# Moving every slot's folds behind the next slot's broadcast of B

## The chip, the cores and the metric

The kernel runs on one core of one Trainium2 chip. The metric is the device time of one execution in microseconds. The five engines are named as the profile names them: PE (TensorE; its weight loads are PEld), DVE (VectorE), ACT (ScalarE), POOL (GpSimd) and SP (SyncE, which here only issues DMAs). Each engine runs its own instructions in order and waits for others through semaphores.

## The reference

Two layers work on x of shape (16, 96, 64, 64), float32. Layer 0 is a graph layer on windows of 8 x 8 positions; layer 1 is two Mamba blocks (selective scans) over the 4,096 positions of each image, followed by a fusion and a batch norm.

```python
# layer 0
y = affine(conv1x1(x, fc1_w, fc1_b), fc1_s, fc1_t)
nodes = window_partition(y, 8).reshape(Bw, C, 64).transpose(0, 2, 1)
idx = knn_idx(nodes, 9)                          # the nine nearest of 64
feat = concat([x_i, x_j - x_i]); h = einsum('bnkc,oc->bnko', feat, ew) + eb
h = max(gelu(h * es + et), axis=2)
x = affine(conv1x1(window_reverse(h), fc2_w, fc2_b), fc2_s, fc2_t) + x
# layer 1, twice: one Mamba block on seq of shape (16, 4096, 96)
h = layernorm(seq); xs, z = split(h @ in_w)      # 192 channels each
xc = silu(causal_conv4(xs) + conv_b)
dt, Bm, Cm = split(xc @ xproj_w)                 # 6, 16, 16
delta = softplus(dt @ dt_w + dt_b)
dA  = exp(delta[..., None] * A)                  # (16, 4096, 192, 16)
dBx = delta[..., None] * Bm[:, :, None, :] * xc[..., None]
hstates[l] = dA[l] * hstates[l - 1] + dBx[l]     # scan over the positions
y = einsum('blds,bls->bld', hstates, Cm) + Dp * xc
seq = seq + (y * silu(z)) @ out_w
# then a fusion product with the pooled mean of x, batch norm, + x
```

## The kernel before

A row is one image's stretch of 512 positions: 16 images times 8 rows. An item is one row in one of the two Mamba blocks, 256 items in all, ordered so that the two blocks alternate (block 1 works four rows behind block 0). The 16 states of an item are taken in eight pairs p = 0 to 7, two states for 64 channels on the 128 partitions, and the 192 channels as three column groups of 512. Item and pair together are one slot: 2,048 slots, numbered m, in one Python loop (line 951). Two items, 16 slots, repeat as a pattern with almost the same work, so a slot is named here by m % 16; p is m % 8. There are 128 patterns.

The order of work on each engine is the order in which the program writes it (a manual schedule). A slot does this for the scan:

- ACT computes da = exp(delta * a) for three column groups (L758, in `chosen`, which also issues the two DMAs that spread the row of C over the partitions into ct, L751). It runs one or two slots ahead, through `ahead`.
- PE spreads the pair's row of B over the partitions, into the one PSUM bank bt (L792, `bcast`). At the top of slot m it does so for slot m + 1. It may not overwrite bt before VectorE has read it.
- DVE scans slot m: hb = da * h + db, in two pieces (L990), and then multiplies u by bt for slot m + 1, giving db (L798, `times_b`, two pieces). There are three hb buffers, so scan m reuses the one of slot m - 3.
- POOL saves the last column (L1024), multiplies hb by ct in place (L1025), and writes the restart value for a later slot into the first column of u (L789).
- PE folds the product of slot m - 1 into y: `folded` (L814 and L816), four matmuls which sum the two states' halves and add to the PSUM tile y over the eight pairs.

y has one buffer. In slot p = 1 ACT copies the last item's finished y out (`emptied`, L823), and PE then starts the new y with the skip product (L808, L809).

Between these, each slot takes steps of other work from generators: layer 0 for a row ahead (L369 to L578), the norm and the products in front of an item (L632 to L734) and behind it (L841 to L861). Their matmuls stand on PE between the broadcast at the top of the slot and the fold at its end. Their PSUM results share one pool of two banks, and ACT reads nearly all of them: each product waits for ACT to free a bank, and ACT waits for the product. Softplus, gelu, silu and exp need table loads on ACT, so its order is also fixed by hand. Every eighth pattern carries the pooled mean of a finished image as well (L590, L597).

In slots p = 1 the fold is already put off: it is kept in `put_off` and issued in slot p = 2, behind that slot's broadcast.

Of the kernel before, what the change touches and what calls it, by code (L numbers as in the profile page):

```python
# [21 lines left out]
def tile_conv_knn_mamba(ctx: ExitStack, tc: tile.TileContext, w: dict, out: bass.AP):  # L22
# [313 lines left out]
    def half(h):  # L336
        return slice(h * CB, (h + 1) * CB)
# [246 lines left out]
    def pooled(b):  # L584

        mean = pr.tile([C, 1], F32, tag="mean1", name=f"mean1_{b}")
        nc.vector.reduce_sum(mean, means.pop(b), AX.X)
        yield
        pg = pm.tile([C, 1], F32, tag="mm", name=f"pg_{b}")
        nc.tensor.matmul(pg, lhsT=gpT, rhs=mean, start=True, stop=True)  # L590
        yield
        gp = pr.tile([C, 1], F32, tag="gp", name=f"gp_{b}")
        nc.scalar.activation(gp, pg, AF.Relu, bias=gp_b[:, 0, :], scale=1.0 / L)
        yield
        def product():
            ps = pm.tile([C, 1], F32, tag="mm", name=f"pg2_{b}")
            nc.tensor.matmul(ps, lhsT=fusT[:, 1, :], rhs=gp, start=True, stop=True)  # L597
            return ps

        apart(product, lambda ps: nc.scalar.copy(gcol[:, b : b + 1], ps))  # L600
        yield


    PIECES = ((0, 2), (2, NB3))
    LAG = 4
    NR = NB * NQ
# [13 lines left out]
    def norm(n):  # L620

        b, i, k = items[n]
        nm = f"{b}_{i}_{k}"
        seq = seqs[b, k]
        assert (b, k) in done
        hn = hns[n % NHN]
        if k == 0:
            nc.gpsimd.memset(hn[:, :HALO], 0.0)
        else:
            nc.gpsimd.tensor_copy(hn[:, :HALO], hns[place[b, i, k - 1] % NHN][:, Q:])  # L630
        pc = pm.tile([C, Q], F32, tag="mm", name=f"pc_{nm}")
        nc.tensor.matmul(pc, lhsT=cmat, rhs=seq, start=True, stop=True)  # L632
        sq = pr.tile([C, Q], F32, tag="sq", name=f"sqv_{nm}")
        nc.scalar.activation(sq, pc, AF.Square)  # L634
        yield
        ps = pm.tile([C, Q], F32, tag="mm", name=f"pvar_{nm}")
        nc.tensor.matmul(ps, lhsT=ones_cc, rhs=sq, start=True, stop=True)
        rs = pr.tile([C, Q], F32, tag="rs", name=f"rs_{nm}")
        nc.scalar.activation(rs, ps, AF.Ln, bias=eps_t[:C], scale=1.0 / C)
        nc.scalar.activation(rs, rs, AF.Exp, scale=-0.5)  # L640
        yield
        nc.gpsimd.tensor_tensor(hn[:C, HALO:], seq, rs, ALU.mult)
# [118 lines left out]
    def carry(n):  # L761

        _, i, k = items[n]
        b0 = made[n][6]
        u, delta = made[n][5], made[n][4]
        fresh = pr.tile([128, NB3, NPR], F32, tag="fresh", name=f"fresh_{n}")
        carried[n] = fresh
        if k:
            first = pr.tile([128, NB3, NPR], F32, tag="first", name=f"first_{n}")
            for c in range(NB3):  # L770
                nc.scalar.activation(first[:, c], a_neg[i][:, c], AF.Exp, scale=delta[:, c, 0:1])
        yield
        nc.gpsimd.tensor_tensor(
            fresh,
            u[:, :, 0:1].to_broadcast([128, NB3, NPR]),
            b0.unsqueeze(1).to_broadcast([128, NB3, NPR]),
            ALU.mult,
        )
        for part in range(2):
            if k:  # L780
                cols = bass.ts(part, NPR // 2)
                nc.gpsimd.tensor_tensor(first[:, :, cols], first[:, :, cols], states[i][:, :, cols], ALU.mult)
                nc.gpsimd.tensor_tensor(fresh[:, :, cols], fresh[:, :, cols], first[:, :, cols], ALU.add)
            yield
            yield
# [5 lines left out]
    def bcast(n, p):  # L791
        nc.tensor.matmul(bt[:, 1:], lhsT=bsel[:, p, :], rhs=made[n][2][:, 1:], start=True, stop=True)  # L792

    def times_b(n, p):
        parts = []
        for lo, hi in PIECES:
            db = pd.tile([128, hi - lo, Q], F32, tag=f"db{lo}", name=f"db{lo}_{n}_{p}")
# [13 lines left out]
    def folded(n, p, hb, y):  # L811

        for h in range(2):
            nc.tensor.matmul(y[half(h), 0], lhsT=fold, rhs=hb[:, h, :], start=False, stop=(p == NPR - 1))  # L814
        for h in range(2):
            nc.tensor.matmul(  # L816
                y[half(h), 1, :QH], lhsT=fold, rhs=hb[:, 2, bass.ts(h, QH)], start=False, stop=(p == NPR - 1)
            )

    def emptied(n, y):  # L820

        yc = zs.popleft()
        nc.scalar.copy(yc, y.rearrange("p s q -> p (s q)")[:, : Q + QH])  # L823
        return yc
# [60 lines left out]
    def several_at_once(g, pace):  # L885

        while True:
            made = 0
            while made < pace:
                step = next(g, g)  # L890
                if step is g:
                    return
                if step in (TABLE, SLOT):
                    break
                made += step is not SPARE
            yield step
# [18 lines left out]
    def ahead():  # L915
        if coming:
            t = coming.popleft()
            soon[t] = chosen(*t)
# [24 lines left out]
    y = behind = None  # L943
# [7 lines left out]
    for m, (n, p) in enumerate(order):  # L951
        b, i, k = items[n]
        nm = f"{b}_{i}_{k}"
        after = order[m + 1] if m + 1 < len(order) else None

        for layer0, r, pace in rows_at.pop(m, ()):
            steps = layer0(*divmod(r, NQ))
            going.append(several_at_once(steps, pace) if pace > 1 else steps)
        between.extend(later[0])
        later = [later[1], []]  # L960
        if p == 0 and k == 0:
            states[i] = pr.tile([128, NB3, NPR], F32, tag=f"state{i}", name=f"state_{nm}")
        if p == 0 and whole:
            going.append(pooled(whole.pop(0)))
        if p == 0 and n + 2 < NI:
            going.insert(0, norm(n + 2))
        if p == 4 and n + 2 < NI:
            preps.append(prelude(n + 2))
        if p == 6 and n + 1 < NI:
            going.append(carry(n + 1))  # L970
        ct, at = soon.pop((n, p))
        if after is not None:
            bcast(*after)
        if p == 2:
            folded(*put_off)


        while uses:
            uses.pop(0)()
        acts = list(opening)  # L980
        opening.clear()
        if not acts and between and p not in (0, 1):
            acts.append(between.popleft())
        if len(acts) > 1:
            acts.pop(0)()
        for act in acts:
            act()
        hb = pr.tile([128, NB3, Q], F32, tag="hb", name=f"hb_{nm}_{p}", bufs=3)
        for (lo, hi), part in zip(PIECES, db):
            nc.vector.tensor_tensor_scan(  # L990
                *(t.rearrange("p c q -> p (c q)") for t in (hb[:, lo:hi], das[at][:, lo:hi], part)), 0.0, ALU.mult, ALU.add
            )
        free.append(at)
        while late:
            if between:
                between.popleft()()
            else:
                late.pop(0)()
        if p == 1 and n:
            yc = emptied(n - 1, y)  # L1000
        if p == 7 and n:
            going.append(tail(n - 1))
        if p == 2:
            ahead()
        held = step_on(going)
        if p == 4:
            ahead()
        held |= step_on(preps)
        close_steps()
        if between and p in (4, 5):  # L1010
            between.popleft()()
        if after is not None:
            if p == NPR - 1:
                restart(*after)
            db = times_b(*after)
        if behind is not None:
            if p == 1:
                y = py.tile([128, 2, Q], F32, tag="y", name=f"y_{nm}")
                skipped(n, y)
                put_off = (*behind, y)  # L1020
            else:
                folded(*behind, y)
        if k + 1 < NQ:
            nc.gpsimd.tensor_copy(states[i][:, :, p : p + 1], hb[:, :, Q - 1 : Q])  # L1024
        nc.gpsimd.tensor_tensor(hb, hb, ct.unsqueeze(1).to_broadcast([128, NB3, Q]), ALU.mult)  # L1025
        if m + 2 < len(order) and p != NPR - 2:
            restart(*order[m + 2])
        if p == 1 and n:
            gate(n - 1, yc)
        behind = (n, p, hb)  # L1030
        while (not held or not soon) and len(soon) < AHEAD and coming:
            ahead()
# [68 lines left out]
```

## Time and profile before

| | |
|---|---|
| median of 3 runs | 12,521.8 us (12,520.07 to 12,522.95) |
| the profiled execution, as timed | 12,521.96 us |
| its span, first to last instruction | 12,520.2 us |
| mean granted TensorE clock | 0.984 |
| DVE: scans L990, products L798 | 6,944.1 us and 3,711.4 us busy |
| POOL: products with C, L1025 | 7,074.4 us busy, 3,454 ns each |
| PE: folds L814 and L816 | 2,179.7 us and 1,244.0 us busy |
| PE: broadcasts L792 | 796.0 us busy, 389 ns each; 180.0 us idle before them |
| DVE's idle time before L798 | 564.1 us |

A row of the timeline gives an instruction's start and length in microseconds, its engine, line and operation, what it writes and reads, and in brackets the engine's idle time before it with what ended it. A line of the waits gives an engine's instruction, what it waited for, the total in microseconds, how often, and the longest. Ends of matmuls are modelled and overlap the next start, so matmuls are measured here from start to start.

### The profile page before, as it was taken

How to read it: one execution, taken by the hardware profiler on the slowest of the kernel's cores; microseconds unless marked ns; L12 is line 12 of the kernel's file. 1: busy time of each engine (PE TensorE's matmuls, PEld its weight loads, DVE VectorE, ACT ScalarE, POOL GpSimd, SP SyncE). 2: the span in 40 equal slices, each digit the busy share in tenths (PEclk: the TensorE clock that was granted, in tenths of full speed). 3: DMA queues.
4: the chain of work that ended last, by engine and by line, in shares of the span. 5: the costliest groups of instructions: out<-in, count | busy, mean ns of one | idle time of the engine just before them, and what ended most of it. 6: DMA issues, size and time to landing. Idle time of an engine off the chain costs nothing. (4 is left out here: it accounts for less than half of the span.)

```text
span 12520.2 us, 169034 instructions
## 1 busy us (share of the span) xinstructions
PE 11019.7 (88%) x50504; PEld 4348.2 (35%) x50504; DVE 11646.8 (93%) x10589; ACT 10249.1 (82%) x16756; POOL 10022.4 (80%) x10148
## 2 busy tenths in 40 slices
PE   7989899898999999899999989989999898998972
PEld 2333333333333333333333333333333333333320
DVE  3999999999999999999999999999999999999995
ACT  6888888888888888888888888888888888888863
POOL 2888888888888888888888888888888888888882
PEclk9999999999999999999999999999999999999996
DMA  1333333333333333333333333333333333333336
GB/s 38 90 86 94 88 90 93 85 92 90 89 92 88 92 91 88 92 91 87 93 89 89 93 86 93 91 89 92 87 93 91 86 93 88 90 93 86 93 92 270
DMA packets 1221003, 1169.01 MB, mean 93 GB/s; under 512 B 631456, under 2 KB 762926, under 8 KB 1213936
## 3 DMA queue, kind: packets, MB, share of 16 engines
q1 hardware_dynamic: 1212720, 1132.88, 33.8%
q10 hardware_dynamic: 7360, 25.32, 0.5%
q8 instruction: 397, 6.50, 0.2%
q14 instruction: 526, 4.31, 0.1%
HBM read 640.79 MB, written 93.09 MB: 59 GB/s over the span
## 5 line engine op out<-in xcount | busy, mean ns | idle before, releaser
L1025 POOL TENSOR_TENSOR hb<-hb,ct 128x1536 f32<-128x1536 f32 x2048 | 7074.4, 3454 | 692.0 <-DMA ct<-cd 448.0
L990 DVE TENSOR_TENSOR_SCAN hb<-da,db 128x1024 f32<-128x1024 f32 (+1 forms) x4096 | 6944.1, 1738 | 4.2 <-ACT da L758 4.2
L798 DVE TENSOR_TENSOR db<-u,bt 128x1024 f32<-128x1024 f32 (+1 forms) x4096 | 3711.4, 952 | 564.1 <-PE bt L792 201.0
L758 ACT ACTIVATE da<-delta,a 128x511 f32<-128x511 f32 x6144 | 3946.1, 710 | 15.9 <-DVE hb L990 8.2
L814 PE MATMUL y<-hb,fold 128*64 128x512 f32 x8192 | 2179.7, 610 | 41.2 <-POOL hb L1025 41.2
L516 ACT ACTIVATE da<-t,eb,es 128x512 f32<-128x512 f32 x1536 | 1168.3, 776 | 714.0 <-PE t L508 453.3
L816 PE MATMUL y<-hb,fold 128*64 128x256 f32 x8192 | 1244.0, 382 | 0.0
L508 PE MATMUL t<-oh,vu 128*128 128x512 f32 x2048 | 1006.4, 613 | 28.2 <-ACT da L516 26.6
L816 PEld LDWEIGHTS y<-hb,fold 128*64 128x64 f32 x8192 | 593.0, 138 | 1191.2 <-issue 1191.2
L1024 POOL COPY state<-hb 128x3 f32<-128x3 f32 x1792 | 374.6, 209 | 766.4 <-DVE hb L990 731.0
L447 DVE TENSOR_REDUCE hq<-da 128x192 f32<-128x1536 f32 x512 | 891.6, 1742 | 91.3 <-ACT da L516 91.3
L792 PE MATMUL bt<-bparts,bsel 128*128 128x511 bf16 x2048 | 796.0, 389 | 180.0 <-DVE db L798 176.6
L659 PE MATMUL pj<-hn,conv_in 128*128 128x512 f32 x2048 | 934.7, 599 | 18.4 <-ACT gcol L600 8.8
L814 PEld LDWEIGHTS y<-hb,fold 128*64 128x64 f32 x8192 | 507.9, 137 | 1078.1 <-issue 695.3
L511 PE MATMUL t<-oh,vu 128*64 128x512 f32 x2048 | 560.8, 626 | 311.6 <-ACT da L516 309.0
L732 POOL TENSOR_TENSOR up<-sp,xc 128x768 f32<-128x768 f32 x256 | 464.1, 1813 | 443.1 <-ACT sp L721 442.9
L664 PE MATMUL pj<-hn,conv_in 128*64 128x256 f32 x4096 | 498.9, 385 | 259.0 <-ACT xc L671 258.8
L671 ACT ACTIVATE xc<-pj,conv_b 128x512 f32<-128x512 f32 (+1 forms) x512 | 297.0, 580 | 425.3 <-PE pj L664 400.4
L477 ACT ACTIVATE oh<-off 64x512 f32<-64x512 bf16 x1024 | 638.2, 623 | 6.4
L492 PE MATMUL pv<-ewT,y 96*64 96x192 f32 x2048 | 447.0, 342 | 143.8 <-ACT sqv L634 83.2
L659 PEld LDWEIGHTS pj<-hn,conv_in 128*128 128x128 f32 x2048 | 378.6, 190 | 406.0 <-issue 368.7
L508 PEld LDWEIGHTS t<-oh,vu 128*128 128x128 f32 x2048 | 371.9, 193 | 394.9 <-issue 298.5
(188 smaller groups left out, 15801.1 us busy)
## 6 DMA issues: line engine op xcount, KB each, us to landing
ct<-cd SPq DMA_DIRECT2D x4096, 128.0 KB
delta<-sp SPq DMA_DIRECT2D x1024, 128.0 KB
u<-up SPq DMA_DIRECT2D x1024, 128.0 KB
delta<-sp SPq DMA_DIRECT2D x1024, 64.0 KB
u<-up SPq DMA_DIRECT2D x1024, 64.0 KB
x<-in_x SPq DMA_DIRECT2D x128, 192.0 KB
rn<-r4d SPq DMA_DIRECT2D x128, 192.0 KB
x_d<-x SPq DMA_DIRECT2D x128, 192.0 KB
```

The lines of the kernel that those rows point to most:

```text
L447: nc.vector.tensor_reduce(out(), g.rearrange("p s (i k) -> p s i k", k=KO), AX.X, ALU.max)
L477: nc.scalar.activation(ohs[p][0:NN, h], off[half(h)], AF.Relu, bias=1.0, scale=-1.0)
L508: nc.tensor.matmul(t, lhsT=vus[p][:, part, :128], rhs=ohw[part], start=True, stop=True)
L516: nc.scalar.activation(g, t, AF.Gelu, bias=e_b[:, j : j + 1], scale=e_s[:, j : j + 1])
L659: nc.tensor.matmul(ps, lhsT=wt[:, t, :128], rhs=hn[:, off : off + Q], start=(t == 0), stop=(t == taps - 1))
L758: nc.scalar.activation(da[:, c, 1:Q], delta[:, c, 1:], AF.Exp, scale=a_neg[i][:, c, p : p + 1])
L792: nc.tensor.matmul(bt[:, 1:], lhsT=bsel[:, p, :], rhs=made[n][2][:, 1:], start=True, stop=True)
L798: nc.vector.tensor_tensor(db, made[n][5][:, lo:hi], bt.unsqueeze(1).to_broadcast([128, hi - lo, Q]), ALU.mult)
L814: nc.tensor.matmul(y[half(h), 0], lhsT=fold, rhs=hb[:, h, :], start=False, stop=(p == NPR - 1))
L816: nc.tensor.matmul(y[half(h), 1, :QH], lhsT=fold, rhs=hb[:, 2, bass.ts(h, QH)], start=False, stop=(p == NPR - 1))
L990: nc.vector.tensor_tensor_scan(*(t.rearrange("p c q -> p (c q)") for t in (hb[:, lo:hi], das[at][:, lo:hi], part)), 0.0, ALU.mult, ALU.add)
L1025: nc.gpsimd.tensor_tensor(hb, hb, ct.unsqueeze(1).to_broadcast([128, NB3, Q]), ALU.mult)
```

## The change

In every slot the fold is kept back and issued in the next slot, behind that slot's broadcast, as it was in slots p = 1 alone. `HASTE` names the slots (m % 16) in which it is kept back, here all of them; the last slot, which has no broadcast after it, folds at once. What the other engines are given, and in which order, is not touched.

```diff
+    HASTE = {0,1,2,3,4,5,6,7,8,9,10,11,12,13,14,15,}
+    put_off = []
     PIECES = ((0, 2), (2, NB3))
...
         if after is not None:
             bcast(*after)
-        if p == 2:
-            folded(*put_off)
-
+        while put_off:
+            folded(*put_off.pop())
...
             if p == 1:
                 y = py.tile([128, 2, Q], F32, tag="y", name=f"y_{nm}")
                 skipped(n, y)
-                put_off = (*behind, y)
-            else:
-                folded(*behind, y)
+            put_off.append((*behind, y))
+            if p != 1 and (m % 16 not in HASTE or after is None):
+                folded(*put_off.pop())
```

## The prediction

> **What bounds the kernel now.** I read the page's busy shares first, then the waits of every engine against every other, then who waits for the scan, and then the timeline of one pattern of 16 slots (the pattern that begins at 6298.03 us), engine by engine. I then took the same rows for all patterns.
>
> The page:
> ```profile
> PE 11019.7 (88%) x50504; PEld 4348.2 (35%) x50504; DVE 11646.8 (93%) x10589; ACT 10249.1 (82%) x16756; POOL 10022.4 (80%) x10148
> ```
> VectorE (DVE) is the busiest at 93%, which by itself would make it the bound. The waits (engine and line, what it waited for, us in total, times, longest) say otherwise:
> ```profile
> ACT da L516 <- PE t L508: 453.3, 281, 3.3
> ACT xc L671 <- PE pj L664: 400.4, 254, 3.0
> ...
> ACT sqv L634 <- PE pc L632: 255.6, 146, 2.0
> PE pj L664 <- ACT xc L671: 259.4, 231, 1.6
> ...
> DVE db L798 <- PE bt L792: 201.0, 131, 11.4
> PE bt L792 <- DVE db L798: 176.6, 190, 3.4
> ```
> ScalarE and TensorE wait for each other for over 1,000 us. Who waits for VectorE's scan (L990)?
> ```profile
>   ACT da L758: 8.2, 3
>   ACT da L516: 5.0, 3
> ```
> ScalarE waited for it 13 us in the whole run. So the loop ScalarE to TensorE to ScalarE hardly looks at VectorE. The rows confirm it. Over 120 patterns (the 3rd to the 122nd of 128) I measured from the first L634 of a pattern to the first gelu of slot 2 (L516): 11.64 us at the 10th, 50th and 90th percentile alike; then to the gelu of slot 3: 4.42, to L721: 4.54, to L671: 6.88 and 2.73, all without spread. 105 patterns, less five with a half-rate TensorE clock, take 93.89 us on average, 93.38 to 93.97 between the 10th and 90th percentile. Every eighth pattern also carries the pooled-mean products (L590, L597) and takes 98.84. VectorE has about 4.2 us of idle time in a pattern before L798: 1.66 in slot 0, 0.89 in slot 3, 0.70 in slot 7, 0.20 in slot 8, 0.60 in slots 11 and 12. That idle time is slack: VectorE is put back in step once a pattern, in slot 7, where L798 waits for GpSimd's restart column, which hangs on ScalarE's L771 and on a transfer of C behind ScalarE's L721.
>
> **The change part by part.** The timeline of TensorE in slots 15 and 0:
> ```profile
> 6298.03 0.38 PE L792 MATMUL bt<-bparts,bsel 128*128 128x511 bf16 x1 [0.51 <-DVE db L798]
> 6298.67 1.10 PE L369 MATMUL pf<-x,fc1T 96*96 96x512 f32 x2 [0.27 <-ACT off L471]
> 6300.02 1.10 PE L557 MATMUL pf<-x,ident 96*96 96x512 f32 x2 [0.25 <-ACT dbl L689]
> ...
> 6305.51 1.08 PE L814 MATMUL y<-hb,fold 128*64 128x512 f32 x4
> 6306.42 0.60 PE L816 MATMUL y<-hb,fold 128*64 128x256 f32 x4
> 6306.95 0.39 PE L792 MATMUL bt<-bparts,bsel 128*128 128x511 bf16 x1
> 6307.18 1.02 PE L632 MATMUL pc<-x,cmat 96*96 96x512 f32 x2
> ```
> Here L369 and L557 wait for ScalarE; the next broadcast comes 1.44 us after the fold begins; L632, for which ScalarE waits 1.95 us, follows. And slots 10 and 11, where slot 10 already has its fold behind the broadcast:
> ```profile
> 6360.07 0.38 PE L792 MATMUL bt<-bparts,bsel 128*128 128x511 bf16 x1 [0.56 <-DVE db L798]
> 6360.38 1.08 PE L814 MATMUL y<-hb,fold 128*64 128x512 f32 x4
> 6361.28 0.60 PE L816 MATMUL y<-hb,fold 128*64 128x256 f32 x4
> 6361.82 1.98 PE L508 MATMUL t<-oh,vu 128*128 128x512 f32 x4
> 6365.26 1.08 PE L511 MATMUL t<-oh,vu 128*64 128x512 f32 x4 [1.46 <-ACT da L516]
> 6366.17 1.03 PE L814 MATMUL y<-hb,fold 128*64 128x512 f32 x4
> 6367.03 0.60 PE L816 MATMUL y<-hb,fold 128*64 128x256 f32 x4
> 6367.56 0.39 PE L792 MATMUL bt<-bparts,bsel 128*128 128x511 bf16 x1
> 6367.79 1.88 PE L508 MATMUL t<-oh,vu 128*128 128x512 f32 x4
> ```
>
> *What moves.* The same four matmuls of a fold change places with one broadcast in 14 of 16 slots; slots 2 and 10 (p = 2) have that order already. Orders on ScalarE, GpSimd and SyncE, and so every DMA issue, stay. VectorE's order stays; 1,789 scans gain a wait for TensorE.
>
> *What is gained.* The broadcast comes 1.39 to 1.44 us earlier (fold start to broadcast start) wherever VectorE is not the one it waits for. That cuts VectorE's idle time in slots 0, 11 and 12. I price it at nothing: what VectorE gains by slot 3 it waits out by slot 7. There L758's second column group ends only 0.48 us (median) before scan 7, and the restart column ends 0.03 us (median) before L798 starts. Both hang on ScalarE. The Trainium skill, Perfetto Trace Analysis, sections Identifying the Most-Contended Engine and Optimization Strategy, says to take the engine of highest occupancy and make what ends its gaps come sooner. By that rule the sum would be the gaps of slots 0, 3, 11 and 12, 3.15 us in 120 patterns, 378 us saved. The rows go against it here.
>
> *The swap itself.* Before: last L511 pass to fold 0.42, fold to broadcast 1.39, broadcast to next 0.23, together 2.04. After, from slots 2 and 10: 0.42, broadcast to fold 0.31, fold to next 1.44, together 2.17. After L846 it is 0.52 + 1.44 + 0.23 = 2.19 against about 2.18. So slot 3, where L508 of the next slot ends ScalarE's wait of 1.69, costs 0.13 us: 120 x 0.13 = 16 us, on the path.
>
> *A broadcast that waits for VectorE with the fold queued behind it.* This is the main cost. The broadcast may start 0.05 us after the L798 pair ends (the row of slot 10). Then come 0.31 and 1.44, so the next product starts at the earliest 1.80 us after that pair ends. Before, the fold ran inside that wait. Call x the time from the end of the L798 pair to the broadcast's start in the trace of before; the next product then started at x + 0.23, so it is late by 1.57 - x.
> - Slot 11: x is 1.21 at the median, and under 1.43 in 65% of the ordinary patterns. L508 is late by 0.44 us on average (the swap's own 0.13 is the least), and ScalarE's gelu waits for it.
> - Slot 8: x is 1.89 at the median; L632 is late in a third of the patterns, 0.15 us on average.
> - Slot 15: the fold goes in front of L369 and L557, which ScalarE releases. L557 can start at 1.80 + 0.94 (L369's two passes) = 2.74 us after the pair ends; it started at 2.50 at the median. Late by 0.30 us on average; L841 to L846, L632 and so ScalarE follow.
> - Slot 9 (x 0.95): late too, but ScalarE's L639 has about 0.5 us to spare there, so slot 11 covers it. Slot 7: L415 waits for ScalarE until after the fold. Elsewhere x is over 1.6.
>
> These don't add: once TensorE is late, the next broadcast waits less. Taking the latest of the three in each pattern gives 0.53 us in 105 patterns and 0.25 in the 15 with pooled means: 55.9 + 3.7 = 60 us. It comes back every pattern, since slot 7 ties VectorE to the late ScalarE again.
>
> *Clock.* The granted clock fell to half in slot 11 for 3.4 or 6.8 us in five of the 105 patterns, where TensorE had been busy for under half of the 3.41 us before. They took 95.5 us, 1.6 more. TensorE will now also stand at slot 11's broadcast, after the 1.46 us before L511; a dozen patterns are within 0.1 of that share. I take six more: 10 us (bounds 0, and 50 patterns: 80 us).
>
> *The new wait of the scan.* Scan m needs the buffer of fold m-3, now behind broadcast m. With the broadcast just in time the fold ends 1.82 us after the broadcast starts, and the scan starts 2.22 after it. Nothing, with 0.4 to spare. Scans 3 and 11 stand so already with no idle time. The y copy (L823) has 0.7 us between its last fold and its start. If either cover goes, the price is the excess: 0.1 us a scan on VectorE's slack, nothing on the path.
>
> *Folds that wait for GpSimd.* Only the last four patterns have them (40.9 us of TensorE's idle time after 11,800 us). There the broadcast no longer stands behind the fold: 4 x 0.7 = 3 us saved.
>
> *Sum.* The profiled execution took 12,521.96 us (span 12,520.2, and 1.8 around it), the median of the runs is 12,521.8. 12,522 + 16 + 60 + 10 - 3 = 12,605 us, 0.66% slower.
>
> **Rivals.**
> - *VectorE is the bound after all, and faster.* For it: 93%, and 201 us of waiting for the broadcast. The place is slot 7: if the restart column comes as much earlier as VectorE does (its product chain starts with the scan of slot 6), the 1.4 us of slot 0 last through the pattern, 120 x 1.4 = 168 us: 12,354; half of it 12,438. Against: the ct transfer and L771 there hang on ScalarE. It decides if L798's wait in slot 7 shrinks.
> - *The lateness is covered.* VectorE reaches slot 8 earlier by part of the 0.70 it waits in slot 7, broadcasts 8, 11 and 15 wait no more, and slots 3 and 11 cost 0.13 each: 120 x 0.26 = 31 us, 12,553; with the swap free, 12,522. For it: x varies by 0.7 to 2.1 in slot 11 (10th to 90th percentile) with that wait.
> - *The clock.* 50 patterns with a half-rate window: 12,675.
> - *The change does less than it says* is out: only slots 2 and 10, and the last fold, keep their places.
>
> **How the numbers follow.** Forecast, 12,555 to 12,670: 0.64. Covered, 12,520 to 12,555: 0.17; about 0.1 of this within 0.2% (25 us, what a measurement of this kernel can tell from no change). Faster: 0.12. Clock, over 12,670: 0.07. The range leaves out the clock case and most of the faster one: 12,510 to 12,670. Faster by over 0.2%: 0.12; within: 0.12; slower: 0.76.
>
> **What would show it.** Right: L798's idle time to the broadcast falls under 100 us; scans, which had 4.2 us, now wait for ScalarE's L758 in slot 7, some 50 to 120 us; TensorE's idle time before L792 rises from 180 to 300 or more; L369 and L557 no longer wait for ScalarE; 105 patterns of 94.4 to 94.7 us; ScalarE's wait in slot 11 for L508 grows. Wrong: the stretch from L557 to L634 and from L516 to L516 in slot 11 keeps its length, or the pattern becomes shorter than 93.9.

## The result, and the profile after

The changed kernel takes 12,723.8 us (median; 12,714.2 to 12,728.3) against 12,520.9 us for the kernel before, measured beside it: a ratio of 1.0161, 95% interval 1.0148 to 1.0173. It is 1.6% slower. The forecast was 12,605 us, 0.66% slower, with a range up to 12,670: the direction was right, the loss was two and a half times as large, and it lies outside the range.

The profiled execution took 12,728.3 us (span 12,726.6, mean granted clock 0.981). Lines move by one or two: the broadcast is now L794, the products of B L800, the fold L816 and L818, the scan L991. From the page, the busy shares and three of its groups:

```profile
PE 11366.1 (89%) x50504; PEld 4252.9 (33%) x50504; DVE 11735.9 (92%) x10589; ACT 10263.4 (81%) x16756; POOL 10015.6 (79%) x10148
...
L991 DVE TENSOR_TENSOR_SCAN hb<-da,db 128x1024 f32<-128x1024 f32 (+1 forms) x4096 | 6941.7, 1736 | 28.6 <-ACT da L760 19.4
L800 DVE TENSOR_TENSOR db<-u,bt 128x1024 f32<-128x1024 f32 (+1 forms) x4096 | 3717.7, 953 | 654.9 <-POOL u L791 342.7
...
L794 PE MATMUL bt<-bparts,bsel 128*128 128x511 bf16 x2048 | 791.8, 387 | 284.6 <-DVE db L800 273.2
```

TensorE does the same 50,504 matmuls, but is busy for 346 us more. The waits (us in total, times, longest) have grown where ScalarE waits for L508 and L634, where the broadcast waits for VectorE, and where VectorE waits for GpSimd's restart column:

```profile
ACT da L516 <- PE t L508: 545.5, 270, 3.9
...
ACT xc L673 <- PE pj L666: 399.0, 254, 2.7
...
DVE db L800 <- POOL u L791: 342.7, 346, 9.1
...
ACT sqv L636 <- PE pc L634: 303.3, 194, 2.7
...
PE bt L794 <- DVE db L800: 273.2, 386, 5.9
...
PE pj L666 <- ACT xc L673: 200.9, 231, 1.3
...
DVE db L800 <- PE bt L794: 154.8, 173, 11.0
```

Before, L508 kept ScalarE for 453 us, L632 (now L634) for 256 and L664 (now L666) for 400, the broadcast waited for VectorE 177, and VectorE waited for the restart column 131. The timeline of TensorE at the place that the prediction shows, slots 15 and 0 of the same pattern:

```profile
6398.44 0.38 PE L794 MATMUL bt<-bparts,bsel 128*128 128x511 bf16 x1 [0.88 <-DVE db L800]
6398.75 1.08 PE L816 MATMUL y<-hb,fold 128*64 128x512 f32 x4
6399.66 0.60 PE L818 MATMUL y<-hb,fold 128*64 128x256 f32 x4
6400.19 1.10 PE L369 MATMUL pf<-x,fc1T 96*96 96x512 f32 x2
6401.12 1.06 PE L557 MATMUL pf<-x,ident 96*96 96x512 f32 x2
```

The broadcast waits for VectorE, the fold stands behind it, and L369 and L557, which used to wait for ScalarE, now start 1.75 and 2.68 us after the broadcast instead of 0.64 and 1.99. Slots 10 and 11:

```profile
6461.86 0.38 PE L794 MATMUL bt<-bparts,bsel 128*128 128x511 bf16 x1 [0.34 <-DVE db L800]
6462.17 1.08 PE L816 MATMUL y<-hb,fold 128*64 128x512 f32 x4
6463.08 0.60 PE L818 MATMUL y<-hb,fold 128*64 128x256 f32 x4
6463.61 1.98 PE L508 MATMUL t<-oh,vu 128*128 128x512 f32 x4
6466.87 1.08 PE L511 MATMUL t<-oh,vu 128*64 128x512 f32 x4 [1.28 <-ACT da L516]
6467.88 0.39 PE L794 MATMUL bt<-bparts,bsel 128*128 128x511 bf16 x1
6468.20 1.08 PE L816 MATMUL y<-hb,fold 128*64 128x512 f32 x4
6469.11 0.60 PE L818 MATMUL y<-hb,fold 128*64 128x256 f32 x4
6469.64 1.99 PE L508 MATMUL t<-oh,vu 128*128 128x512 f32 x4
```

No wait stands between L511 and the second L508, and still they are 2.77 us apart (6466.87 to 6469.64); before it was 2.53 (6365.26 to 6367.79). L508 itself takes 1.99 instead of 1.88. ScalarE, at the same place, waits for it 1.68 us before (first row) and 2.03 us after (second and third):

```profile
6368.85 1.64 ACT L516 ACTIVATE da<-t,eb,es 128x512 f32<-128x512 f32 x2 [1.68 <-PE t L508]
...
6468.00 0.78 ACT L516 ACTIVATE da<-t,eb,es 128x512 f32<-128x512 f32 x1 [0.51 <-PE t L511]
6470.81 1.64 ACT L516 ACTIVATE da<-t,eb,es 128x512 f32<-128x512 f32 x2 [2.03 <-PE t L508]
```

**Where the 206 us are** (difference of the two spans; a pattern is counted here from one broadcast at the top of slot 0 to the next): the 105 ordinary patterns 141.7 (93.97 to 95.31 us each), the 15 patterns with pooled means 40.8 (98.84 to 101.57), the last six patterns and the end 22.3, the start 1.5. Within a pattern the difference sits in a few stretches between events on ScalarE and TensorE; every stretch not in this table keeps its length to within 0.1 us. The stretches are means over the ordinary patterns, in us; the columns after the second are experiments told below. In a pattern with pooled means the stretch to the gelu of slot 11 alone grew by 1.72 (7.62 to 9.34).

| stretch | before | after | only 2, 10 | all but 2, 10 | only 7, 8, 14 | early fold |
|---|---|---|---|---|---|---|
| gelu of slot 2 to gelu of slot 3 | 4.42 | 4.77 | 4.77 | 4.42 | 4.42 | 3.13 |
| L689 of slot 7 to L634 of slot 8 | 6.78 | 7.02 | 6.78 | 6.98 | 6.97 | 6.79 |
| to the gelu of slot 10 | 11.77 | 11.94 | 11.77 | 11.91 | 11.88 | 11.74 |
| to the gelu of slot 11 | 4.48 | 4.86 | 5.11 | 4.51 | 4.48 | 3.38 |
| first L689 to the second pass of L557, slot 15 | 1.32 | 1.52 | 1.32 | 1.47 | 1.51 | 1.32 |
| ordinary pattern | 93.97 | 95.31 | 94.95 | 94.51 | 94.41 | 91.55 |
| pattern with pooled means | 98.84 | 101.57 | 99.49 | 100.22 | 100.24 | 96.92 |

(Lines by the numbering of before. ScalarE's L634 is the square that reads the product L632.)

### The profile page after: what moved, and what is told of

It reads as the page before. It is cut to its first block, busy times and chain, and to the rows that moved or that the text cites. A ratio compares the mean times of both kernels' runs of the same rounds, so it can differ in the third digit from the quotient of the medians.

```text
span 12726.6 us, 169159 instructions
## 1 busy us (share of the span) xinstructions
PE 11366.1 (89%) x50504; PEld 4252.9 (33%) x50504; DVE 11735.9 (92%) x10589; ACT 10263.4 (81%) x16756; POOL 10015.6 (79%) x10148
## 4 chain that ended last, share of the span: by engine, by line
ACT 26%; PE 25%; POOL 11%; DVE 11%; SPq 10%; issue 8%; DMA 8%; POOLq 0%; ACTq 0%; DVEq 0%
ACT da L760 10%; POOL hb L1026 9%; DVE hb L991 5%; DMA ct<-cd 4%; DVE db L800 4%; SPq L744 3%; PE y L816 3%; PE t L511 3%; SPq L742 3%; PE t L508 3%; SPq L753 2%; DVE hq L447 2%; DMA r4d<-r 2%; ACT da L516 2%; PE y L818 1%
## 5 line engine op out<-in xcount | busy, mean ns | idle before, releaser
L991 DVE TENSOR_TENSOR_SCAN hb<-da,db 128x1024 f32<-128x1024 f32 (+1 forms) x4096 | 6941.7, 1736 | 28.6 <-ACT da L760 19.4
L800 DVE TENSOR_TENSOR db<-u,bt 128x1024 f32<-128x1024 f32 (+1 forms) x4096 | 3717.7, 953 | 654.9 <-POOL u L791 342.7
L816 PE MATMUL y<-hb,fold 128*64 128x512 f32 x8192 | 2245.8, 627 | 3.2 <-POOL hb L1026 3.2
L818 PE MATMUL y<-hb,fold 128*64 128x256 f32 x8192 | 1249.7, 384 | 0.0
L508 PE MATMUL t<-oh,vu 128*128 128x512 f32 x2048 | 1034.3, 627 | 35.2 <-ACT da L516 33.6
L794 PE MATMUL bt<-bparts,bsel 128*128 128x511 bf16 x2048 | 791.8, 387 | 284.6 <-DVE db L800 273.2
L818 PEld LDWEIGHTS y<-hb,fold 128*64 128x64 f32 x8192 | 596.1, 139 | 1196.9 <-issue 1196.9
L511 PE MATMUL t<-oh,vu 128*64 128x512 f32 x2048 | 566.4, 632 | 348.2 <-ACT da L516 345.4
L816 PEld LDWEIGHTS y<-hb,fold 128*64 128x64 f32 x8192 | 408.5, 136 | 1127.4 <-issue 858.8
L666 PE MATMUL pj<-hn,conv_in 128*64 128x256 f32 x4096 | 498.5, 385 | 200.5 <-ACT xc L673 200.4
L1025 POOL COPY state<-hb 128x3 f32<-128x3 f32 x1792 | 343.1, 191 | 328.9 <-DVE hb L991 322.0
L492 PE MATMUL pv<-ewT,y 96*64 96x192 f32 x2048 | 446.2, 341 | 96.6 <-ACT sqv L636 83.3
L508 PEld LDWEIGHTS t<-oh,vu 128*128 128x128 f32 x2048 | 348.9, 191 | 493.2 <-issue 411.5
```

The lines of the kernel that those rows point to most:

```text
L508: nc.tensor.matmul(t, lhsT=vus[p][:, part, :128], rhs=ohw[part], start=True, stop=True)
L511: nc.tensor.matmul(t[half(h)], lhsT=vus[p][:, h, 128:], rhs=ohw[h], start=True, stop=True)
L800: nc.vector.tensor_tensor(db, made[n][5][:, lo:hi], bt.unsqueeze(1).to_broadcast([128, hi - lo, Q]), ALU.mult)
L818: nc.tensor.matmul(y[half(h), 1, :QH], lhsT=fold, rhs=hb[:, 2, bass.ts(h, QH)], start=False, stop=(p == NPR - 1))
L991: nc.vector.tensor_tensor_scan(*(t.rearrange("p c q -> p (c q)") for t in (hb[:, lo:hi], das[at][:, lo:hi], part)), 0.0, ALU.mult, ALU.add)
```

## The experiments

Three theories stood against each other. A: the loop of ScalarE and TensorE sets the pace, and what a fold delays there is the loss. B: VectorE sets it. C: TensorE's clock does.

### The moves apart

The set `HASTE` names the slots whose fold is kept back; a fold kept back in slot s changes places with the broadcast at the top of slot s + 1. Four runs each change this one line of the changed kernel:

```diff
-    HASTE = {0,1,2,3,4,5,6,7,8,9,10,11,12,13,14,15,}
+    HASTE = {2,10,}                                  # only_2_10
+    HASTE = {0,1,3,4,5,6,7,8,9,11,12,13,14,15,}      # all_but_2_10
+    HASTE = {7,8,14,}                                # only_7_8_14
+    HASTE = {15,}                                    # only_15
```

> Only the folds of slots 2 and 10 move (behind the broadcasts of slots 3 and 11, which follow L511). Theory A, the loop between ScalarE and TensorE sets the pace and the changed order itself makes TensorE's stretch from L511 to the next L508 longer: 0.35 us in slot 3 and 0.35 to 0.45 us in slot 11 of 120 patterns, 85 to 95 us, and up to 2 us in each of the 15 patterns with pooled means: 85 to 125 us slower than before. Theory B, VectorE sets the pace and loses time only where all folds are moved (scans that wait for folds, restart columns): broadcasts 4 and 12 come up to 1.1 us earlier, so 0 to 100 us faster. Theory C, the half-rate clock windows: under 20 us slower.

> All folds move but those of slots 2 and 10. Theory A: what is left of the 203 us, 80 to 120 us slower than before; the stretches between the gelus of slots 2 and 3 and of slots 10 and 11 are back at 4.42 us. Theory B: the whole 203 us or nearly, since most scans still wait for folds. Theory C: the half-rate windows of slot 11 go back to before's, some 180 us slower or less.

> Only the folds in front of broadcasts 8, 9 and 15 move: the three places where the broadcast waits for VectorE with the fold queued behind it. Theory A: L632 of slot 8, L637 of slot 9 and L557 of slot 15 are late by 0.2 us each on average, 40 to 75 us slower than before. Theory B: those broadcasts were not what VectorE waited for, so within 20 us of before. Theory C: within 20 us of before.

> Only the fold of slot 15 moves, behind broadcast 0, for which VectorE waits longest in before (1.66 us in slot 0). Theory A: VectorE's idle time in slot 0 falls by over 1 us and comes back in slots 3 to 7; the time is within 15 us of before. Theory B: the 1.1 to 1.4 us last, 120 to 170 us faster. Theory C: as before.

Measured, beside 12,522.8 us for the kernel before:

| run | median, us | ratio, 95% interval | more, us |
|---|---|---|---|
| only 2, 10 | 12,629.7 | 1.0087 (1.0072 to 1.0102) | 107 |
| all but 2, 10 | 12,623.5 | 1.0080 (1.0065 to 1.0095) | 101 |
| only 7, 8, 14 | 12,591.2 | 1.0055 (1.0039 to 1.0072) | 68 |
| only 15 | 12,526.6 | 1.0004 (0.9995 to 1.0013) | 4 |

All four are where A put them. Half of the loss is the two moves in front of the products L508, of slots 3 and 11; two thirds of the other half are the three places where a broadcast waits for VectorE. The first two runs share out all moves, and 107 and 101 add up to the 203 of the whole within 5 us. The last run is B's: it cuts VectorE's idle time in front of the products of B from 1.66 to 0.25 us in slot 0, and the idle time comes back in slots 1 (0 to 0.48) and 3 (0.89 to 1.83); nothing is gained. C falls as the main cause with the first run: its trace has 21 half-rate clock windows in the 120 patterns, before's has 19, and still 107 us are lost.

### What the swap itself costs

The stretch from the last product in front, over fold and broadcast, to the next product (start to start; medians over the 120 patterns, the table has those without a wait inside) changed by nearly the same amount wherever the products in front and behind were of the same kind:

| product in front, columns of TensorE it uses | before, us | after, us |
|---|---|---|
| L511 (slots 3, 11), 64 | 2.04 | 2.29 |
| L717 (4), 64 | 1.83 | 2.07 |
| L717 (12, with L431 behind), 64 | 1.92 | 2.07 |
| L664 (6, 14), 64 | 1.83 | 2.08 |
| L493 (1), 64 | 1.78 | 2.02 |
| L846 (0, 8), 96 | 2.19 | 2.18 |
| L659 (5, 13), 128 | 2.19 | 2.18 |

Medians of single steps (start to start, between matmuls with no wait between them) say what it depends on. After a pass of 512 elements on 64 columns, a product on 64 columns starts 0.42 us later (L511 to the fold, before), one on 128 columns 0.52: L511 to the broadcast, after, 0.525, and L511 to L523, in the trace of before, 0.522. From L846 or L659 to the fold it is 0.52, to the broadcast 0.43. A step between narrow and wide costs about 0.1 us, in either direction. The fold is narrow (64), the broadcast wide (128). Behind L511 the order before, narrow, narrow, wide, wide (L511, fold, broadcast, L508), has one such step; the order after, narrow, wide, narrow, wide, has three. Behind L846 both orders have two. That gives 0.2 and 0, against 0.245 and -0.01 measured. The first pass of L508 also takes 0.533 us behind a fold and 0.429 behind a broadcast; its other three take 0.429 either way, with the change of weights between its two products among them. So slots 3 and 11 pay 0.35.

Columns alone don't say it all. L431, which follows in slot 12, has 64 columns like the fold but 64 rows instead of 128, and it comes 0.31 us after the last pass of the fold, as a wide product does, where from L664 or L717 to the fold (128 rows and 64 columns on both sides) it is 0.21. So going from 128 to 64 rows costs the step too, as far as this one pair shows; from 96 to 128 rows (L493 to the fold, 0.156, as from one L493 to the next L492) it costs nothing.

A first idea was that it matters whether the fold's first half stands on the same 64 columns as the product in front or on the others. The halves of each fold were turned:

```diff
-        for h in range(2):
+        for h in (1, 0):
             nc.tensor.matmul(y[half(h), 0], ...
```

> The order of before, with the two halves of every fold taken in the order 1, 0. L511, the last product in front of the fold, writes the upper or lower 64 columns alone. If the place of the columns decides whether the fold's weights load beneath L511 (theory D): L511 to fold 0.52 us instead of 0.42, slots 3 and 11 each 0.1 longer, 24 us slower, 12,547. If it is only the width of 64 columns: 0.42 as before, and 12,522.

It took 12,523.2 us, a ratio of 1.0000 (0.9990 to 1.0011), and the stretch after L511 stayed at 2.04. Which half comes first doesn't matter; the rows above leave the width. The number format is not it: the step from L511 is the same to L523, which is f32, and to the broadcast, which is bf16. Why the step costs time, the weight load or something else, was not tried.

### Is VectorE's idle time slack?

```diff
+        if m % 16 == 1:
+            nc.vector.memset(idle, 0.0)
```

> The kernel before with one more instruction on VectorE in slot 1 of every pattern, a memset of 128x512 f32 (about 0.5 us) whose result nobody reads. Theory A: VectorE waits 0.89 us for the broadcast in slot 3, so the half microsecond is taken up there: within 15 us of before. Theory B: 128 x 0.49 = 62 us slower, 12,584.

It took 12,521.9 us, a ratio of 0.9999 (0.9989 to 1.0009): 128 instructions of 485 ns, 62 us of work on the engine that is busy 93% of the time, cost nothing. VectorE's idle time in slot 3 fell from 0.89 to 0.37 us, by the half microsecond, and no other changed by more than 0.03. B falls.

### Does the fold cover a late VectorE?

The same memset was put where it makes VectorE's products of B in front of the broadcast of slot 11 later, in the kernel before and in the changed one (`m % 16 == 10`, ahead of the scan).

> The kernel before with one memset of 128x512 f32 on VectorE (0.485 us, as it measured in the run with the load in slot 1) ahead of the scan in the iteration whose products of B and the broadcast release the broadcast of slot 11. In the trace of before that broadcast starts 1.21 us (median, 0.52 at the 5th percentile) after VectorE's pair ends, because the fold stands in front of it. Theory A (the fold is the cover): the half microsecond disappears under the fold, 0 to 15 us slower: 12,522 to 12,537. Theory B (VectorE sets the pace): 62 us slower, 12,584.

> The same memset at the same place in the changed kernel. There the broadcast of slot 11 starts 0.28 us (median, 0.13 at the 5th percentile) after VectorE's pair ends, with the fold behind it. Theory A: some 0.2 to 0.45 us of the 0.485 go through to the products L508 and to ScalarE's gelu in each pattern: 25 to 55 us slower than the changed kernel, 12,750 to 12,780. If the cover isn't the cause of the waiting: within 15 us of the changed kernel, 12,709 to 12,739.

Before: 12,521.9 us, ratio 0.9999 (0.9990 to 1.0008), as A expected. The delay did arrive there: the broadcast starts 0.80 us after VectorE's pair (median) instead of 1.21. After: 12,727.8, ratio 1.0162 (1.0147 to 1.0177), which is 4 us more than the changed kernel without it and not the 25 to 55 expected. The timeline of slot 11 there shows the mechanism at work (the broadcast is L795):

```profile
6458.59 1.08 PE L512 MATMUL t<-oh,vu 128*64 128x512 f32 x4 [1.27 <-ACT da L517]
6459.99 0.38 PE L795 MATMUL bt<-bparts,bsel 128*128 128x511 bf16 x1 [0.33 <-DVE db L801]
6460.30 1.08 PE L817 MATMUL y<-hb,fold 128*64 128x512 f32 x4
```

The broadcast that waited for nothing now waits 0.33 us, with the fold behind it, and the stretch to the gelu of slot 11 grows from 4.86 to 5.17, by 0.31 us. But the other places take some of it back: the stretches to L634 of slot 8, to the gelu of slot 10 and to L557 become shorter by 0.04, 0.06 and 0.07, since ScalarE is later and VectorE isn't. The ordinary pattern takes 95.47 instead of 95.31, 16 us in 105 patterns, with 13 half-rate clock windows in them instead of 8. And the 15 patterns with pooled means take 13 us less together: they had 20 such windows instead of 29 (see below). The cover and its loss are shown at their place; that they fix the whole time is not. The waits partly replace one another.

### The clock

Patterns with pooled means, sorted by how many windows of 3.41 us at half the clock they had: before, seven patterns with none take 97.66 us, four with one 99.29, four with two 100.47. So a window costs 1.2 to 1.6 us. After, none is without: two have one, twelve have two (101.56), one has three. That is 12 windows before and 29 after, nearly all beginning between the broadcasts of slots 10 and 11; in the ordinary patterns there are 7 and 8. The count differs from one execution to the next: the five traces whose time is that of before have 9 to 18 in the patterns with pooled means, and the two with all folds moved have 29 and 20. So part of the 17 more may be chance. Busy time of each engine and granted clock (PEclk) around there, after:

```profile
5309.40:5312.80 3.40, 1.14 (x3) 0.31 (x3) 3.40 (x6) 3.09 (x4) 3.40 (x5) 0.99 0.00 0
5312.80:5319.60 6.80, 5.93 (x13) 1.08 (x14) 5.75 (x8) 1.70 (x3) 6.30 (x5) 0.50 0.00 1
```

and in the same pattern before, at the same distance from the broadcast of slot 11:

```profile
5224.60:5228.00 3.40, 1.80 (x8) 0.44 (x4) 3.40 (x5) 3.37 (x5) 3.40 (x4) 1.00 0.11 38
5228.00:5234.80 6.80, 5.74 (x21) 2.04 (x23) 6.80 (x11) 2.78 (x6) 6.27 (x6) 1.00 0.00 1
```

After, TensorE was busy for 1.14 of 3.40 us while it waited for ScalarE's gelu, and the clock fell to half for the next two windows; before, with 1.80 of 3.40, it did not. All thirteen traces say the same when each stretch at full clock is cut into windows of 3.41 us, back from the next fall, leaving out the first and last 400 us: of some 44,000 windows, those in which TensorE was busy for less than 0.4 were all followed by half clock, and none with more than 0.65 was; the falls and the exceptions overlap between 0.42 and 0.63.

### The fold where TensorE is idle anyway

If A is right, the fold does not belong behind the broadcast of slots 3 and 11, nor in front of it, but in the 1.3 us for which TensorE waits for ScalarE ahead of L511. Here, starting from the kernel before, the fold of slots p = 2 is handed to the generator of layer 0, which issues it there:

```diff
                 for part in range(3):
+                    if part == 2 and early:
+                        early.pop()()
                     t = pm.tile([128, Q], F32, tag="mm", ...)
...
+        if p == 2:
+            early.append(partial(folded, *behind, y))
         held = step_on(going)
...
-            else:
+            elif p != 2:
                 folded(*behind, y)
+            elif early:
+                early.pop()()
```

> The order of before, except that in the slots with p = 2 (slots 2 and 10 of a pattern) the fold of the slot in front is issued between the two products L508 and the product L511, where TensorE stands idle for 1.34 to 1.46 us because it waits for ScalarE's gelu. Theory A (the loop of ScalarE and TensorE sets the pace): the 1.7 us of fold leave the path in front of the products of slots 3 and 11, less what the fold now delays L511 itself (0.3 us or so); about 2.0 to 2.4 us a pattern in slots 3 and 11 together, 200 to 290 us faster than before: 12,230 to 12,320. VectorE then has little idle time left. Theory B (VectorE sets the pace): only the 0.89 us for which it waits for the broadcast in slot 3 and 0.3 in slot 11 can go, at most 120 us: 12,400 or more.

It took 12,230.2 us, a ratio of 0.9767 (0.9752 to 0.9782): 295 us faster. B allowed at most 120. In slot 2 (here the fold is L817 and L819, L511 and L514 are the products L508 and L511):

```profile
6171.17 1.98 PE L511 MATMUL t<-oh,vu 128*128 128x512 f32 x4
6173.09 1.08 PE L817 MATMUL y<-hb,fold 128*64 128x512 f32 x4
6174.00 0.60 PE L819 MATMUL y<-hb,fold 128*64 128x256 f32 x4
6174.50 1.08 PE L514 MATMUL t<-oh,vu 128*64 128x512 f32 x4
6175.51 0.39 PE L795 MATMUL bt<-bparts,bsel 128*128 128x511 bf16 x1
6175.74 1.88 PE L511 MATMUL t<-oh,vu 128*128 128x512 f32 x4
```

The idle time is gone from in front of L514. The stretch to the gelu of slot 3 falls from 4.42 to 3.13 and the one in slot 11 from 4.48 to 3.38; the pattern takes 2.42 us less. The half-rate windows go with the idle time: none is left in the ordinary patterns, six in those with pooled means.

With the fold of slot 15 behind the broadcast of slot 0 on top of it:

> The early fold in slots 2 and 10, and the fold of slot 15 behind the broadcast of slot 0 (the part of the change that alone cost nothing, 12,526.6). If the early fold leaves VectorE as the bound, the 1.4 us that it no longer waits in slot 0 last through the pattern: up to 100 us faster than the early fold alone. If ScalarE and TensorE still set the pace: within 20 us of it.

12,237.3 us, ratio 0.9773 (0.9759 to 0.9788): no gain: VectorE's idle time in slot 0 fell from 0.96 to 0.08 us and came back mostly in slots 1 and 7, so VectorE, busy 95% of the time in the early fold, is still not the bound. Last, on top of the early fold, the fold ahead of the broadcasts of slots 0 and 8 was moved behind the product L632, for which ScalarE waits:

```diff
         nc.tensor.matmul(pc, lhsT=cmat, rhs=seq, start=True, stop=True)
+        while delayed:
+            delayed.pop()()
...
+            elif p == 7 and after is not None:
+                delayed.append(partial(folded, *behind, y))
```

> The early fold in slots 2 and 10, and the fold in front of the broadcasts of slots 0 and 8 moved behind them and behind L632, the product for which ScalarE waits 1.94 us in slot 0. In the trace of the early fold TensorE stands 0.68 us idle in front of the next products (L492) there. Theory A: the products of slot 0 come 0.6 to 0.7 us sooner, those of slot 8, where ScalarE doesn't wait for L632, 0 to 0.3: 60 to 120 us faster than the early fold, 12,110 to 12,170, unless VectorE, now at 95%, takes the gain back. Theory B: no faster than the early fold, 12,215 to 12,245.

12,204.7 us, ratio 0.9743 (0.9727 to 0.9759), the fastest of all; 25 us less than the early fold alone where 60 to 120 were expected. L632 and the square behind it come 0.76 us sooner, but the stretch from there to the gelu of slot 2 grows from 11.64 to 12.18, because the fold now stands ahead of L492. A fold in front of one product that ScalarE needs was exchanged for a fold in front of the next.

## Why the prediction was half right

The direction and the main places of the loss were right, its size was not: the prediction failed in the terms "the swap itself" and "these don't add", and in two smaller ones, the clock and the folds that wait for GpSimd.

- *What sets the pace.* Right. The loop of ScalarE and TensorE does; two loads on VectorE (a memset in slot 1, one in front of slot 11) and one gift to it (the broadcast of slot 0 sooner) moved the kernel before by no more than 4 us. "I price it at nothing" held, and the rival that VectorE is the bound fell.
- *"The swap itself", 0.13 us in slot 3.* This is a step that failed by size: 0.35, so 42 us and not 16 in 120 patterns. The 0.42 from L511 to the next matmul was taken over from L511 to the fold, where both are narrow; the broadcast is wide, and the trace of before had that case (L511 to L523, 0.522). And L508 at 1.98 behind a fold, against 1.88 behind a broadcast, stood in the rows that the prediction shows, unused. The same 0.35 is the least that slot 11 loses.
- *"These don't add", the latest of three, 0.53 us.* The main cost was named rightly, with its three places, and mis-sized: together the stretches of slots 8 to 11 and 15 lose 0.24 + 0.17 + 0.38 + 0.20 = 0.99 us in an ordinary pattern, 104 us and not 56. They are not independent, as the run with both kinds of moves against each alone shows (slot 11 loses 0.63 alone and 0.38 with the others), but they come nearer to a sum than to a maximum. Their own means in the prediction, 0.15, 0.44 and 0.30, had added to 0.89. The 0.17 up to the gelu of slot 10 is a place priced at nothing: slot 9, where L639 was to have 0.5 us to spare and slot 11 to cover the rest. L639 starts 0.20 us later behind L634 and now waits for L637, 18 us in the whole run against 7.
- *"Clock", 10 us.* The mechanism was right and its place wrong. Of 18 windows more in this pair of traces, 17 are in patterns with pooled means, which the count of near misses had left out. At 1.2 to 1.6 us a window these are 20 to 27 us, some of it perhaps chance. What else these patterns lost was 8 to 15 us beside slot 3, where 4 were priced.
- *"Folds that wait for GpSimd", -3 us.* Wrong in sign: the last six patterns and the end lost 22. The waits in the last 310 us in front of the final eight slots, before:

```profile
PE bt L792 <- DVE db L798: 39.8, 31, 3.4
POOL up L732 <- ACT sp L721: 20.0, 7, 3.6
...
DVE db L798 <- POOL u L789: 16.8, 10, 2.8
...
ACT sqv L634 <- PE pc L632: 6.8, 6, 2.0
```

and after, in 316 us:

```profile
PE bt L794 <- DVE db L800: 72.0, 38, 5.9
...
POOL up L734 <- ACT sp L723: 34.7, 7, 5.8
DVE db L800 <- POOL u L791: 31.6, 10, 5.1
...
ACT sqv L636 <- PE pc L634: 15.5, 6, 2.7
```

  The fold no longer waits for GpSimd, as forecast; but now the broadcast waits for VectorE, ScalarE for L634 behind it, GpSimd for ScalarE, and VectorE for GpSimd. The loss came whole with all moves but those of slots 2 and 10 (22 us) and not with 7, 8 and 14 alone (4) or 15 alone (4); which of the remaining ones it takes was not tried.
- *The new wait of the scan* cost nothing that shows, as priced: the scans' idle time rose by 24 us, and none of it is put down to a fold. 19.4 us of their idle time is for ScalarE, where 50 to 120 were forecast as a sign; VectorE waits in front of L800 instead, 343 us for GpSimd's restart column.
- *What would show it.* Of the two stretches that were to grow, the one between the gelus up to slot 11 did (4.48 to 4.86). The one from L557 to L634 kept its length (8.22 and 8.21 us): what slot 15 loses is lost in front of L557, so this sign was badly chosen. TensorE's idle time ahead of the broadcast grew (180 to 285, 300 forecast), as did ScalarE's wait for L508 (453 to 546). TensorE's idle time for ScalarE in front of L369 fell from 83 to 8 us, in front of L557 only from 26 to 15. The ordinary pattern of 95.31 us lies above the 94.4 to 94.7 forecast, and L800's idle time to the broadcast fell to 155 and not under 100.

Added up: 42 for slot 3, 104 for the waits in the ordinary patterns, 35 for the rest of those with pooled means, 22 at the end and 1.5 at the start are 205 of the 206 us.

## What to carry to other kernels

Before an operation is moved past another, count at both places what it will stand next to, and take each step's time from a row with the same pair of shapes, not from the same first instruction. An in-order engine that waits makes all that is queued behind it wait: what used to run inside the wait (here the fold) should not be moved behind it, and the best place for it is an idle stretch that another engine causes (2.3% here, against a loss of 1.6% for the move as made). The busiest engine is not the bound until an instruction added to it costs time.

## What the runs showed of the hardware

- Start to start, a step from a matmul on 64 columns to one on 96 or 128, or back, costs about 0.1 us more than one between equals (0.52 against 0.42 or 0.43 after a pass of 512 f32 elements), and the first pass of an f32 product of 128 columns behind one of 64 another 0.1 (0.533 against 0.429). Which half of the columns is used makes no difference (12,523.2 us with the halves turned).
- The clock fell to half after windows of 3.41 us in which TensorE was not idle but busy for too little of the time: in the thirteen traces always under 0.4, never over 0.65. A window of 3.41 us at half rate cost 1.2 to 1.6 us here, and work moved into the idle stretch took most of these windows away (from 19 to 6 in 120 patterns).
